# A two-layer graph network on one core: layer 1's projection bias and the experts' gated last biases move from TensorE to VectorE

## The chip, the core and the metric

The kernel runs on one core of a Trainium2 chip. A core has a matrix engine (TensorE, PE in the profile, with its weight loads listed as PEld), a vector engine (VectorE, DVE), a scalar engine (ScalarE, ACT), GpSimd (POOL) and a queue engine (SyncE, SP). Each works through its own list of instructions in order; semaphores make one wait for another. Data lies in main memory (DRAM), in the on-chip memory SBUF (128 partitions) and, for the results of TensorE, in the banks of PSUM. Transfers are issued from SP, ACT or POOL. The metric is the device time of one execution in microseconds (us); lower is better.

## What is computed

Two layers, each of a graph convolution, an attention mix and a feed-forward part, over 3,125 nodes with 256 features and 100,000 edges. The change lies in the second layer ("layer 1"). What matters of the reference there, shortened:

```
xn = layernorm(x)
x  = x + gnn(xn) + mix(xn)
x  = x + experts(layernorm(x))

mix:      y   = second-order attention of 8 heads over all nodes
          mix = y @ Wproj.T + bproj                       # bproj: 256 numbers
experts:  w   = softmax(xl @ Wr + br)                     # 8 gates for each node
          h1  = relu(bn1(xl @ W1[e] + b1[e]))             # for each expert e of 8
          h2  = relu(bn2(h1 @ W2[e] + b2[e]))
          out = sum over e of  w[e] * (h2 @ Wo[e] + bo[e])    # bo: 8 x 256 numbers
```

All of it is in four-byte floating point. `bproj` and `bo` are not zero in the inputs used.

## The kernel before

The nodes lie in 25 tiles of 128 rows (the last has 53), and most loops go over chunks of four tiles (`CHUNKS`; seven, the last of a single tile). The kernel lays the edges out as dense matrices of counts, so that each aggregation over the graph is a product with a 3,125 x 3,125 matrix on TensorE. Layer 1 starts at about 1,300 us. Three of its stages matter here.

*The second aggregation with the queries* (from `layer1_middle`, the block of pools `mid_2`, about 1,700 to 2,023 us). `conv_rows` (L875 to L898) multiplies the matrix's columns, loaded from DRAM on SP's queue (L832) and cast by ScalarE (L835), with the features `hs` that stay in SBUF (L888, 128x512 products). Between these products the generator `queries` (L2085) is advanced step by step by `before(k)`: for each of two groups of heads it multiplies two streams `left` and `right` on VectorE (L2107; both are loaded on POOL's queue at L2082, with 1 MB each) and takes the results to TensorE (L2116). A denominator goes the way L2095, L2098 (VectorE, `ns`), L2099 (ScalarE), L2111 (TensorE, `bp`), L2113 (VectorE, a reciprocal). L2118 puts a group together in `oT`, and then, for each tile, L2125 multiplies with the projection weights into a PSUM bank `yp`, L2126 adds the bias to the same bank, and L2127 adds the bank to the node's row `xc` in SBUF. `xc` was loaded at the chunk's start (L2203, SP's queue). At the end of a chunk `row_sums` (L901, with L906, L907 and L909) adds the aggregation to `xc`, and L2220 stores it.

*The experts' preparation* (`prepare`, L1886). For a chunk it loads `xc` (L1891), normalizes it (L165 to L180), turns it into columns on TensorE (L191 to L195) and computes the eight gates (L1900 to L1917). Then, for each tile, `weighted_bias` (L1039) adds the gated biases: a transpose of the gates on TensorE (L1042), a copy by ScalarE (L1044), a product of the transposed gates with the eight rows `bo` (L1046), and an addition to `xc` by VectorE (L1047). The first chunk is prepared ahead, inside the aggregation's last chunks; the others each during the experts of the chunk before, two steps of the generator per expert from the second expert on.

*The experts* (`experts1`, L1924, from about 2,023 us to the end). Here the chunks are four of four tiles and three of three. For each chunk and each of eight experts: two layers of products over columns (L1952) with ScalarE's activation (L1957), then for each tile a product with the last weights (L1968) into one of three banks, and VectorE's L1971, which multiplies the bank by the tile's gate and adds it to `xc`. At the chunk's end L1977 stores `xc` as the result.

The order on each engine comes from the compiler, which goes by the order of writing and by its own estimate of when an instruction's inputs are there; an instruction whose inputs are there early can be placed far ahead of where it is written. Memory of a pool that has ended is reused, and an instruction that writes there waits for the last reader of the tile that lay there. The weights of experts 1 to 7 are loaded on SP's queue (L1863) when the aggregation's memory comes free.

`bo` is loaded by `common` (L1866) on ACT's queue as 8 rows of 256 numbers; `bproj` lies in `rows`, a block that was copied to all 128 partitions at the start (L1482), and L2126 uses one partition of it.

Of the kernel before, what the change touches and what calls it, by code (L numbers as in the profile page):

```python
# [7 lines left out]
F32 = mybir.dt.float32  # L8
# [4 lines left out]
OP = mybir.AluOpType  # L13
# [4 lines left out]
P = 128  # L18
# [80 lines left out]
def tile_gps_layers(ctx: ExitStack, tc: tile.TileContext, a: dict, out: bass.AP):  # L99
# [1766 lines left out]
    def common(fp):  # L1866

        w_r = load_w(fp, "f1_wr", 2)
        bo = fp.tile([NE1, C], F32, name="bo")
        nc.scalar.dma_start(bo, a["f1_bo"])  # L1870

        bn = []
        for i in "12":
            v = fp.tile([P, 16], F32, name="bn_v" + i)
            DVE.tensor_scalar(v, col("v" + i), 1e-3, None, op0=OP.add)
            sc = fp.tile([P, 16], F32, name="bn_s" + i)
            rsqrt_v(fp, sc, v, [P, 16], "bn" + i)
            DVE.tensor_mul(sc, sc, col("g" + i))
            bi = fp.tile([P, 16], F32, name="bn_b" + i)
            DVE.tensor_sub(bi, col("b" + i), col("m" + i))  # L1880
            DVE.tensor_mul(bi, bi, sc)
            DVE.tensor_add(bi, bi, col("be" + i))
            bn.append((sc, bi))
        return w_r, bo, bn

    def prepare(fw, psp, tag, queue, ts, w_r, bo, got, spare=None):  # L1886


        n = len(ts)
        xc = fw.tile([P, 4, C], F32, name="xc", bufs=1 if spare else 3)  # L1890
        queue.dma_start(xc[:, :n], x_dram[ts[0]:ts[0] + n].rearrange("t p c -> p t c"))  # L1891
        xn = layernorm(fw, [xc[:, i] for i in range(n)], xn=spare and spare())
        yield
        xT = fw.tile([P, 2, 512], F32, name="xT")
        to_columns(psp, tag, xn, ts, xT)
        yield
        gp_ = psp.tile([P, 512], F32, name="gp_", tag=tag)
        for i in range(n):
            for k in range(2):
                PE.matmul(  # L1900
                    gp_[:, i * 8:(i + 1) * 8], xT[:, k, i * P:(i + 1) * P], w_r[:, k, :],
                    start=k == 0, stop=k == 1,
                )
        gate = fw.tile([P, 4, NE1], F32, name="gate")
        ga = gate[:, :n]
        DVE.tensor_add(
            ga, gp_[:, :n * 8].rearrange("p (t e) -> p t e", e=8),
            row("f1_br")[:, None, :].to_broadcast([P, n, 8]),
        )
        red = fw.tile([P, 4], F32, name="red")  # L1910
        DVE.tensor_reduce(red[:, :n], ga, AX.X, OP.max)
        DVE.tensor_sub(ga, ga, red[:, :n, None].to_broadcast([P, n, 8]))
        ACT.activation(ga, ga, AF.Exp)
        yield
        DVE.tensor_reduce(red[:, :n], ga, AX.X, OP.add)
        DVE.reciprocal(red[:, :n], red[:, :n])
        DVE.tensor_mul(ga, ga, red[:, :n, None].to_broadcast([P, n, 8]))  # L1917
        got[:] = xT, gate, xc
        yield
        for i, t in enumerate(ts):  # L1920
            weighted_bias(psp, tag, fw, gate[:, i, :], NE1, bo, xc[:, i])
            yield

    def experts1(pre):  # L1924

        with pool("ffn", **right) as fp, pool("ffn_w", bufs=2, **right) as fw, pool("ps_f", bufs=3, space=PSUM) as ps, \
                pool("ps_fp", bufs=2, space=PSUM) as psp:
            now = []
            chunks = CHUNKS[:4] + [list(range(t, t + 3)) for t in range(16, NT, 3)]
            if pre:  # L1930
                (w_r, bo, bn), got, ws = pre
            else:
                w_r, bo, bn = common(fp)
                got, ws = [], [expert(fp, 0, nc.sync)]
                for _ in prepare(fw, psp, "p", nc.sync, chunks[0], w_r, bo, got):
                    pass
            ws = ws + [expert(fp, e, nc.sync) for e in range(1, NE1)]
            for c, ts in enumerate(chunks):
                xT, gate, xc = got
                w = sum(rows_of(t) for t in ts)  # L1940
                got = []
                ahead = iter(())
                if c + 1 < len(chunks):
                    ahead = prepare(fw, psp, "p", nc.sync, chunks[c + 1], w_r, bo, got)
                for e in range(NE1):
                    h = xT
                    for layer in range(2):
                        hn = fw.tile([P, 2, 512], F32, name=f"h{layer}")
                        for f in range(2):
                            hp = ps.tile([P, 512], F32, name="hp", tag="h")  # L1950
                            for k in range(2):
                                PE.matmul(  # L1952
                                    hp[:, :w], ws[e][layer][:, k, f * P:(f + 1) * P], h[:, k, :w],
                                    start=k == 0, stop=k == 1,
                                )
                            at = 2 * e + f
                            ACT.activation(  # L1957
                                hn[:, f, :w], hp[:, :w], AF.Relu,
                                bias=bn[layer][1][:, at:at + 1], scale=bn[layer][0][:, at:at + 1],
                            )  # L1960
                        h = hn
                    if e:
                        turns(ahead, 2)
                    for i, t in enumerate(ts):
                        r = rows_of(t)
                        yp = ps.tile([P, 512], F32, name="yp", tag="y")
                        for k in range(2):
                            PE.matmul(  # L1968
                                yp[:r, :C], h[:, k, i * P:i * P + r], ws[e][2][:, k, :], start=k == 0, stop=k == 1
                            )  # L1970
                        DVE.scalar_tensor_tensor(  # L1971
                            xc[:r, i], yp[:r, :C], gate[:r, i, e:e + 1], xc[:r, i], op0=OP.mult, op1=OP.add
                        )
                for _ in ahead:
                    pass
                r0, full = ts[0] * P, [t for t in ts if rows_of(t) == P]
                stores = [nc.sync.dma_start(  # L1977
                    out[r0:r0 + len(full) * P, :].rearrange("(t p) c -> p t c", p=P), xc[:, :len(full)]
                )]
                if len(full) < len(ts):  # L1980
                    stores.append(nc.sync.dma_start(out[(NT - 1) * P:N, :], xc[:LAST, len(full)]))
                for o in stores:
                    after(o, stored)
                now.extend(stores)
            stored.extend(now)

    def layer1(fast, rest):
        with pool("l1", **right) as lp:
# [96 lines left out]
            def queries(qw, lq, pst, ps, ts, xc, early):  # L2085
# [3 lines left out]
                for g in range(2):  # L2089
# [15 lines left out]
                    for m in range(4):  # L2105
                        qq = qw.tile([P, 4 * 512], F32, name="qq", bufs=2)
                        DVE.tensor_mul(qq[:, :4 * w], left[m % 2], right[m // 2])  # L2107
                        yield
                        if m == 0:
                            bp = ps.tile([P, 512], F32, name="bp", tag="a")  # L2110
                            PE.matmul(bp[:, :w], sel, ns[:, :w], start=True, stop=True)  # L2111
                            rden = qw.tile([P, 512], F32, name="rden", bufs=1)
                            DVE.reciprocal(rden[:, :w], bp[:, :w])  # L2113
                        for h in range(4):
                            s = slice(h * HD, (h + 1) * HD)
                            PE.matmul(acc[s, :w], kvp[:, g, m, s], qq[:, h * w:(h + 1) * w], start=False, stop=m == 3)  # L2116
                        yield
                    DVE.scalar_tensor_tensor(  # L2118
                        oT[:, g, :w], acc[:, :w], vs[:, g:g + 1], rden[:, :w], op0=OP.add, op1=OP.mult
                    )  # L2120
                    yield
                for i in range(n):
                    yp = ps.tile([P, 512], F32, name="yp", tag="a")
                    for g in range(2):
                        PE.matmul(yp[:, :C], oT[:, g, i * P:(i + 1) * P], wpr[:, g, :], start=g == 0, stop=False)  # L2125
                    PE.matmul(yp[:, :C], ones[0:1, :], row("m1_bproj")[0:1, :], start=False, stop=True)  # L2126
                    DVE.tensor_add(xc[:, i], yp[:, :C], xc[:, i])  # L2127
                    yield

            def layer1_middle(fast, rest, left_, pre):  # L2130
                with pool("mid", **right) as ch, pool("mid_a", bufs=2, **right) as ca:
# [58 lines left out]
                    with pool("mid_2", **right) as cw, pool("ps_c2", space=PSUM) as psc, \  # L2190
# [7 lines left out]
                        for ts in CHUNKS:  # L2198
# [8 lines left out]
                            if fast and ts is CHUNKS[5]:  # L2207
# [1 line left out]
                                made = common(fp)  # L2209
                                got, ws = [], [expert(fp, 0, nc.scalar)]  # L2210
                                spare = lambda: cw.tile([P, 4, C], F32, name="xc", bufs=2)
                                early_work.append(prepare(fp, ps, "a", nc.scalar, CHUNKS[0], *made[:2], got, spare))
                                pre.extend((made, got, ws))
                            acc = conv_rows(ca, psc, hs, ts, fast, gen, before)
                            for _ in work:
# [70 lines left out]
```

## Time and profile before

| | |
|---|---|
| median of 3 runs | 2601.89 us (2598.73 to 2609.38) |
| profiled execution | 2595.34 us, of which the span of the instructions is 2593.4 us |
| mean granted TensorE clock | 0.970 |
| from 2046 us to the end: L1968, L1952 on TensorE | 774 records, 188.4 us; 864 records, 351.0 us |
| the same: L1971 on VectorE | 195, 92.7 us, 482 ns each |
| the same: L1046 on TensorE | 42 records, 14.6 us |
| the same: L1047 on VectorE | 21, 8.9 us, 425 ns each |
| L2126 on TensorE, 1746.4 to 2020.9 us | 50 records, 374 to 791 ns, median 478 |

The times of the runs are of executions without a profile; the profiled execution is another one, and sums made from the trace are compared with its own time. A product of four-byte numbers shows as two records on TensorE, each with a weight load; records of consecutive products overlap, so the time that a product holds TensorE is read from the starts, not from the sum of the durations. In lists of groups, `out<-in` names the tiles written and read, and idle time is put down to what ended it ("<-PE yp L1968": the engine waited for that product).

### The profile page before, as it was taken

What the parts mean: (1) busy time and instruction counts of PE and PEld (TensorE: products, weight loads), DVE (VectorE), ACT (ScalarE), POOL (GpSimd) and SP (SyncE); (2) the same over time, 40 slices, a digit from 0 to 9 for tenths busy, and PEclk for the clock granted to TensorE, in tenths of its full rate; (3) what the DMA queues carried; (4) which work ended last, traced back from release to release, by engine and by line L of the source; (5) the groups of instructions that cost most, each with busy time, mean ns of one, the idle gap of its engine ahead of it and who ended that gap; (6) DMA issues with size and microseconds to landing.
All of it is one profiled execution on the core that took longest, in us unless ns stands there. A gap on an engine that the chain in (4) does not pass through costs nothing.

```text
span 2593.4 us, 33233 instructions
## 1 busy us (share of the span) xinstructions
PE 2442.5 (94%) x12351; PEld 1531.6 (59%) x12351; DVE 1545.2 (60%) x3534; ACT 1382.0 (53%) x2356; POOL 145.2 (6%) x203
## 2 busy tenths in 40 slices
PE   5788999989997999999999899989999999999998
PEld 3466777666674545555564576755555555555665
DVE  5689976548848777766778565566775412222221
ACT  5756766569858898777745334343332232222332
POOL 5320000000000000000001000001110000000000
PEclk9899999989997899999999999998999999999999
DMA  6434444366643211111146644387873400000000
GB/s 192 137 102 154 162 160 154 128 204 240 225 133 107 68 51 56 57 57 48 51 140 220 223 150 136 94 297 265 295 286 116 130 8 1 15 15 9 8 5 13
DMA packets 197059, 318.44 MB, mean 123 GB/s; under 512 B 12461, under 2 KB 171510, under 8 KB 190742
## 3 DMA queue, kind: packets, MB, share of 16 engines
q1 hardware_dynamic: 177110, 246.11, 29.2%
q0 software_dynamic: 14592, 64.28, 7.0%
q10 hardware_dynamic: 5184, 5.82, 0.7%
q8 instruction: 99, 1.62, 0.3%
q14 instruction: 74, 0.61, 0.1%
HBM read 229.40 MB, written 86.73 MB: 122 GB/s over the span
## 4 chain that ended last, share of the span: by engine, by line
PE 66%; DMA 5%; DVE 4%; ACT 3%; issue 1%; POOL 0%; ACTq 0%; DVEq 0%; SPq 0%; POOLq 0%
PE hp L1952 13%; PE acc L888 9%; PE yp L1968 7%; PE yp L1132 7%; PE hp L1118 6%; PE acc L862 6%; PE qa L2038 2%; PE by_s L1284 2%; PE tt L2116 2%; DMA adj<-cols 2%; PE wb_p L1046 1%; PE by_a L1282 1%; PE b_bank L419 1%; DMA xs_n<-hs_dram 1%; ACT adj_r L835 1%
## 5 line engine op out<-in xcount | busy, mean ns | idle before, releaser
L835 ACT CAST adj_r<-adj 128x2560 fp32r<-128x2560 bf16 (+1 forms) x140 | 293.6, 2104 | 303.2 <-PE acc L862 114.1
L888 PE MATMUL acc<-hs,adj_r 128*128 128x512 f32 (+1 forms) x1250 | 360.1, 421 | 14.4 <-ACT adj_r L835 11.6
L1957 ACT ACTIVATE h<-hp,bn_b,bn_s 128x512 f32<-128x512 f32 (+2 forms) x224 | 160.9, 723 | 368.6 <-PE hp L1952 368.6
L862 PE MATMUL acc<-adj_r,hs 128*128 128x512 f32 (+1 forms) x1400 | 353.9, 395 | 0.5 <-ACT adj_r L835 0.5
L1271 ACT ACTIVATE pos<-drow,a_s 128x512 bf16<-128x512 f32 (+2 forms) x532 | 311.5, 665 | 0.9 <-PE by_s L1284 0.5
L888 PEld LDWEIGHTS acc<-hs,adj_r 128*128 128x128 f32 (+1 forms) x1250 | 226.8, 190 | 114.7 <-issue 55.9
L1971 DVE SCALAR_TENSOR_TENSOR xc<-yp,gate,xc 128x256 f32<-128x256 f32 (+1 forms) x200 | 95.1, 482 | 320.5 <-PE yp L1968 320.3
L862 PEld LDWEIGHTS acc<-adj_r,hs 128*128 128x128 f32 x1400 | 245.9, 191 | 55.6 <-issue 8.3
L1118 PE MATMUL hp<-g_xT,w 128*128 128x512 f32 (+2 forms) x448 | 199.1, 563 | 1.9 <-issue 1.6
L1132 PE MATMUL yp<-w,hT 128*128 128x256 f32 x800 | 196.3, 387 | 0.0
L1968 PE MATMUL yp<-w_f_wo,h 128*128 128x256 f32 (+1 forms) x800 | 194.7, 386 | 0.3 <-ACT h L1957 0.2
L1275 DVE TENSOR_TENSOR pos<-pos,adj 128x2048 bf16<-128x2048 bf16 (+2 forms) x133 | 147.0, 1105 | 67.9 <-ACT pos L1271 67.6
L1952 PE MATMUL hp<-h,w_f_w 128*128 128x512 f32 (+2 forms) x448 | 185.8, 545 | 0.3
L2029 DVE TENSOR_TENSOR kk<-vk 128x512 f32<-128x512 f32 (+1 forms) x200 | 125.3, 687 | 99.1 <-issue 51.6
L436 ACT CAST b_stage<-b_bank 128x500 bf16<-128x500 f32 (+8 forms) x363 | 169.2, 534 | 27.6 <-PE b_bank L419 25.9
L1952 PE MATMUL hp<-xT,w_f_w 128*128 128x512 f32 (+2 forms) x448 | 181.9, 544 | 1.6 <-issue 1.6
L390 DVE TENSOR_TENSOR b_ul<-lo_b,upto 128x2048 bf16<-128x2048 bf16 x117 | 148.9, 1273 | 48.3 <-PE b_bank L419 48.0
L1968 PEld LDWEIGHTS yp<-w_f_wo,h 128*128 128x128 f32 (+1 forms) x800 | 142.6, 187 | 49.8 <-ACT h L1957 14.5
L1132 PEld LDWEIGHTS yp<-w,hT 128*128 128x128 f32 x800 | 147.8, 191 | 40.6 <-issue 20.0
L419 PE MATMUL b_bank<-b_uh,b_ul 128*128 128x125 bf16 (+5 forms) x1856 | 138.7, 214 | 17.6 <-DVE b_uh L395 10.4
L419 PEld LDWEIGHTS <-b_ul 128*128 128x128 bf16 x1856 | 101.8, 100 | 67.4 <-issue 48.8
L1952 PEld LDWEIGHTS hp<-h,w_f_w 128*128 128x128 f32 x448 | 81.6, 189 | 94.0 <-issue 38.8
(563 smaller groups left out, 3382.1 us busy)
## 6 DMA issues: line engine op xcount, KB each, us to landing
adj<-cols SPq DMA_DIRECT2D x145, 640.0 KB, 4.4
cols<-b_stage SPq DMA_DIRECT2D x50, 800.0 KB, 3.6
left<-q_dram POOLq DMA_DIRECT2D x22, 1024.0 KB
right<-q_dram POOLq DMA_DIRECT2D x20, 1024.0 KB
xs_n<-hs_dram SPq DMA_DIRECT2D x15, 640.0 KB, 5.5
vk<-vk_dram SPq DMA_DIRECT2D x10, 840.0 KB, 5.5
vk_dram<-vk SPq DMA_DIRECT2D x6, 1344.0 KB, 4.9
x_in<-in_x SPq DMA_DIRECT2D x12, 512.0 KB, 3.9
```

Of the source, the lines that this page charges most:

```text
L390: DVE.tensor_tensor(u, lo[:, s].rearrange("p (m j) -> p m j", j=2)[:, :, None, :].to_broadcast([P, group // 2, P, 2]), upto[:, None, :P, : ...
L419: PE.matmul(bank[:, n * NT:(n + w) * NT], u[:, i // 2, :, i % 2], v[:, i // 2, :NT * w, i % 2], start=k == 0, stop=k == room - 1,)
L436: ACT.copy(dst, src)
L835: ACT.copy(dst, src)
L862: PE.matmul(acc[f][:, :w], hs[:, k, q, s], at[k - k0][:, :len(ts)], start=k == 0 and q == 0, stop=k == NT - 1 and q == 1,)
L888: PE.matmul(acc[i][:r, :], at[k - k0][:, i, :r], hs[:, k].rearrange("p q c -> p (q c)"), start=k == 0, stop=k == NT - 1,)
L1118: PE.matmul(hp[:, :w], w1[:, e, k, f * P:(f + 1) * P], xT[:, k, c0:c0 + w], start=k == 0, stop=k == 1)
L1132: PE.matmul(yp[:, :C], hT[:, f, i * P:(i + 1) * P], w2[:, e, f, :], start=f == 0, stop=f == 3)
L1271: ACT.activation(pos[:, h, :n].rearrange("p t d -> p (t d)"), drow[:, h, :w], AF.Sign, bias=a_s[:, k, h:h + 1],)
L1952: PE.matmul(hp[:, :w], ws[e][layer][:, k, f * P:(f + 1) * P], h[:, k, :w], start=k == 0, stop=k == 1,)
L1957: ACT.activation(hn[:, f, :w], hp[:, :w], AF.Relu, bias=bn[layer][1][:, at:at + 1], scale=bn[layer][0][:, at:at + 1],)
L1968: PE.matmul(yp[:r, :C], h[:, k, i * P:i * P + r], ws[e][2][:, k, :], start=k == 0, stop=k == 1)
```

## The change

Two biases are no longer products.

The projection bias: the product L2126 goes, so that L2125 alone fills the bank. In its place VectorE adds the 256 numbers of `bproj`, which lie in every partition of `rows`, to all tiles of the chunk's `xc` in one operation, written after the first group's last product and ahead of its L2118.

The gated biases: the loop over `weighted_bias` at the end of `prepare` goes. `bo` is now loaded in `experts1` on POOL's queue as one row of 8 x 256 numbers copied to all 128 partitions (8 KB in each), as the first tile of the experts' pool. Before each expert's products VectorE multiplies the bias row of the expert before with its gate and adds it to `xc`, one operation for each tile; the last expert's turn adds its own row too.

```diff
     def common(fp):
         w_r = load_w(fp, "f1_wr", 2)
-        bo = fp.tile([NE1, C], F32, name="bo")
-        nc.scalar.dma_start(bo, a["f1_bo"])
...
     def prepare(fw, psp, tag, queue, ts, w_r, got, spare=None):
...
         got[:] = xT, gate, xc
         yield
-        for i, t in enumerate(ts):
-            weighted_bias(psp, tag, fw, gate[:, i, :], NE1, bo, xc[:, i])
-            yield
 
     def experts1(pre):
...
+            bo = fp.tile([P, NE1, C], F32, name="bo")
+            nc.gpsimd.dma_start(
+                bo.rearrange("p e c -> p (e c)"),
+                a["f1_bo"].rearrange("(o e) c -> o (e c)", o=1).to_broadcast([P, NE1 * C]),
+            )
...
                 for e in range(NE1):
+                    for b in {0: (), NE1 - 1: (e - 1, e)}.get(e, (e - 1,)):
+                        for i in range(len(ts)):
+                            DVE.scalar_tensor_tensor(
+                                xc[:, i], bo[:, b], gate[:, i, b:b + 1], xc[:, i], op0=OP.mult, op1=OP.add
+                            )
                     h = xT
...
+                    if not g:
+                        DVE.tensor_add(xc[:, :n], xc[:, :n], row("m1_bproj")[:, None, :].to_broadcast([P, n, C]))
                     DVE.scalar_tensor_tensor(
                         oT[:, g, :w], acc[:, :w], vs[:, g:g + 1], rden[:, :w], op0=OP.add, op1=OP.mult
                     )
...
                     for g in range(2):
-                        PE.matmul(yp[:, :C], oT[:, g, i * P:(i + 1) * P], wpr[:, g, :], start=g == 0, stop=False)
-                    PE.matmul(yp[:, :C], ones[0:1, :], row("m1_bproj")[0:1, :], start=False, stop=True)
+                        PE.matmul(yp[:, :C], oT[:, g, i * P:(i + 1) * P], wpr[:, g, :], start=g == 0, stop=g == 1)
                     DVE.tensor_add(xc[:, i], yp[:, :C], xc[:, i])
```

The rest of the diff passes `bo` no longer from `common` to `prepare` and `experts1`.

More of the change, by code (lines that the diff above doesn't have):

```diff
@@ L1883, in common, with prepare @@
             bn.append((sc, bi))
-        return w_r, bo, bn
-    def prepare(fw, psp, tag, queue, ts, w_r, bo, got, spare=None):
+        return w_r, bn
+    def prepare(fw, psp, tag, queue, ts, w_r, got, spare=None):
         n = len(ts)
@@ L1929, in experts1 @@
             chunks = CHUNKS[:4] + [list(range(t, t + 3)) for t in range(16, NT, 3)]
+            bo = fp.tile([P, NE1, C], F32, name="bo")
[3 more added lines that the diff above has]
+            )
             if pre:
-                (w_r, bo, bn), got, ws = pre
+                (w_r, bn), got, ws = pre
             else:
-                w_r, bo, bn = common(fp)
+                w_r, bn = common(fp)
                 got, ws = [], [expert(fp, 0, nc.sync)]
-                for _ in prepare(fw, psp, "p", nc.sync, chunks[0], w_r, bo, got):
+                for _ in prepare(fw, psp, "p", nc.sync, chunks[0], w_r, got):
                     pass
@@ L1943, in experts1 @@
                 if c + 1 < len(chunks):
-                    ahead = prepare(fw, psp, "p", nc.sync, chunks[c + 1], w_r, bo, got)
+                    ahead = prepare(fw, psp, "p", nc.sync, chunks[c + 1], w_r, got)
                 for e in range(NE1):
+                    for b in {0: (), NE1 - 1: (e - 1, e)}.get(e, (e - 1,)):
[3 more added lines that the diff above has]
+                            )
                     h = xT
@@ L2211, in layer1_middle @@
                                 spare = lambda: cw.tile([P, 4, C], F32, name="xc", bufs=2)
-                                early_work.append(prepare(fp, ps, "a", nc.scalar, CHUNKS[0], *made[:2], got, spare))
+                                early_work.append(prepare(fp, ps, "a", nc.scalar, CHUNKS[0], made[0], got, spare))
                                 pre.extend((made, got, ws))
```

## The prediction

> **What bounds the kernel now.** I read the page's busy shares first, then the stretches of the two stages that the change touches, then the chain of work, and last the single lines. The page:
>
> ```profile
> PE 2442.5 (94%) x12351; PEld 1531.6 (59%) x12351; DVE 1545.2 (60%) x3534; ACT 1382.0 (53%) x2356; POOL 145.2 (6%) x203
> ```
>
> The share is an average, so the stages decide. Busy time by stretch (start:end, length, then PE, PEld, DVE, ACT, POOL, clock, DMA share, GB/s); the first two are chunks of layer 1's second aggregation, the last two lie in its experts:
>
> ```profile
> 1852.15:1900.52 48.37, 48.37 (x205) 26.41 (x205) 32.72 (x26) 15.42 (x13) 5.74 (x10) 1.00 0.80 286
> 1900.52:1948.89 48.37, 48.37 (x206) 26.40 (x205) 32.63 (x26) 15.42 (x13) 5.73 (x10) 1.00 0.75 275
> 2100.00:2200.00 100.00, 99.88 (x317) 55.36 (x316) 20.14 (x47) 28.82 (x41) 0.00 (x0) 1.00 0.02 6
> 2200.00:2300.00 100.00, 99.89 (x312) 54.31 (x310) 22.84 (x64) 29.38 (x42) 0.00 (x0) 1.00 0.03 10
> ```
>
> TensorE never rests in either stage; VectorE is busy 68% in the aggregation and 20 to 23% in the experts. Work taken from TensorE there is time, work given to VectorE is time only where TensorE waits for it. The chain of the experts (start, duration, piece) starts an expert every 10.87 us (2178.09 to 2188.96 to 2199.83), but 12.52 to 12.56 us where bias steps lie in it:
>
> ```profile
> 2153.01 4.29 PE hp L1952 x10
> ...
> 2165.53 4.29 PE hp L1952 x10
> ...
> 2178.09 4.29 PE hp L1952 x10
> ...
> 2188.96 4.29 PE hp L1952 x10
> ...
> 2199.83 4.29 PE hp L1952 x10
> ```
>
> The same chain close up shows what the extra time is:
>
> ```profile
> 2160.15 0.11 PE wb_t L1042
> 2160.26 1.46 PE yp L1968 x6
> 2161.72 0.62 PE wb_p L1046 x2
> 2162.34 0.20 PE wb_t L1042
> 2162.55 0.43 PE yp L1968 x2
> 2162.98 0.62 PE wb_p L1046 x2
> ```
>
> The projection bias, in TensorE's order of one chunk (each product of four-byte numbers is two records):
>
> ```profile
> 1893.12 1.02 PE L2125 MATMUL yp<-w_m_wproj,oT 128*128 128x256 f32 x4
> 1894.07 0.69 PE L2126 MATMUL yp<-rows,ones 1*128 1x256 f32 x2
> 1894.70 0.50 PE L888 MATMUL acc<-hs,adj_r 128*128 128x512 f32 x1
> ```
>
> L2126 holds TensorE from 1894.07 to 1894.70, 0.63 us, though it has one row.
>
> **The change part by part.** Time removed in the experts: L1042, L1044, L1046, L1047 for 21 tiles after 2023. Chunks of four tiles prepare a chunk of four in two experts of 12.52 and 12.56 instead of 10.87 us: 3.34 us, three times, 10.0. The fourth prepares three tiles: its two experts run from 2337.23 to 2361.44, 24.21 less 21.74, 2.5 us. A chunk of three tiles takes 7.75 us per expert without bias; from 2402.45 to 2469.69 it took 67.24 us, less 62.0, less 0.66 for transposes and 1.24 for gates, leaves 3.3, of which I count 3.2, twice: 6.4. Together 18.9 us, all on a chain that is TensorE's alone.
>
> The first chunk's four bias steps run in the aggregation, near 1989 to 2005, 0.62 and 0.11 us each: 2.9 us.
>
> The projection bias is 25 products. The chain's own list for 1745 to 2023 (278 us) gives L2126 4.6%, that is 12.8 us: 17 at 0.62, two at 1.15 in a stretch of slow clock. The other six lie in the first two chunks, where the chain goes through a load of the matrix (17.22 us from 1737.81) and one of POOL's (12.02 us from 1781.28); I count them as nothing, since those loads hide them. If that cover is gone they are worth 6 x 0.62 = 3.7 us. Next behind L2125 stand L888, which waited for its casts 3.3 us in this whole stage, and L2127, which now waits for L2125. A tile of this loop goes from 1.92 to 1.29 us, against 0.42 us of L2127, so the two banks of yp don't hold it.
>
> Removed: 12.8 + 2.9 + 18.9 = 34.6 us.
>
> Added, (a): seven additions of the projection bias, six over 1,024 elements per partition. The rows of the same kind are 0.42 us at 256 (L907), 0.69 at 512 and 2.29 at 2,048 (L2107): a line through the last two gives 1.22 us. Written just ahead of L2118, but the trace runs VectorE's work well ahead of its place: the layernorm that is written in the sixth chunk ran at 1787, in the second. So the addition goes to a gap after the load of xc, a chunk ahead (issued 1867.31, 1915.64). Gaps of 2.5 to 3.4 us before L2113 hold it for nothing. If it falls between L2118 and L2098 instead, it delays ns, for which TensorE already waits:
>
> ```profile
> PEld bp L2111 <- ACT ns L2099: 4.8, 7, 0.8
> ```
>
> (line, what is waited for, us in total, times, longest). Then up to 1.2 us a chunk are lost: ends 0 and 7.3 us. I take 0.9 in two chunks of six, 1.8, being nearer to the gaps, which are longer than the work. The four L1047 that go here give VectorE back 1.7 us.
>
> (b): the eight bias rows copied to all partitions, 1 MB on POOL's queue in place of 8 KB on ACT's (0.38 us of ACT's issue, hidden). It is the first tile of the experts' memory, where hs lay, so it waits for the last L888 at 2021.87; POOL's last load before it is issued at 2012.56 and nothing is queued behind it. The nearest rows: a row block copied to all partitions at the start, 836 KB, landed in 8.4 us, which makes 10.5 for 1 MB; POOL's own 1 MB took 12.02. So it lands at 2032 to 2034; the first addition that needs it follows L1971 of expert 0, at 2034.7. At best it costs nothing. At worst it shares the queues until the burst of weights ends (5.4 MB and 1.5 MB of xc, 350 GB/s until 2044, with 1 MB more until 2047): VectorE stands for 12 us, L1971 behind it frees no bank and TensorE stands at the fourth yp. The same megabyte makes xc of the next chunks land up to 2.9 us later, and there TensorE waited already 0.36 us for ln_xn at 2052. I take 1.5 us, half of that, since the likelier lands in time.
>
> (c): 200 additions over 256 elements, 0.42 (L907) to 0.48 us (L1971), 90 us of VectorE in 562. In an expert of 10.87 us there are then 1.9 us of L1971 and 1.9 us of these (3.8 in the last expert), and 5 us of layernorm in one of eight. Between two yp of 0.93 us VectorE has at worst 1.44 us of work, so it falls 1.5 us behind over four tiles, and TensorE needs the next bank 7 us later. Nothing on the path; if that cover were gone, it is 0.5 us in each of the 56 experts, 28 us. Each addition waits for gate and xc, both there since L1971 of the expert before; queued behind it stand L1971 and the next layernorm. TensorE's loads and ScalarE's 21 copies L1044 go for nothing, being beside TensorE.
>
> Sum: 34.6 - 1.8 - 1.5 = 31.3 us. The profiled execution took 2595.3 us (span 2593.4), so it would be 2564.0. That execution lies 6.6 us under the median of the runs, 2601.9; against the median I forecast **2570 us**.
>
> [...] Row first: POOL's issues of left and right take 0.53 to 0.55 us whether L2107, an operation with two inputs from SBUF, is running (1839.45) or not (1783.47). [...]
>
> **The rivals.** 1: slower or nothing gained. The additions (a) run ahead to where the compiler thinks xc has landed, and VectorE stands in order until it has. For it speaks a row of today, where a layernorm that ran ahead did this:
>
> ```profile
> 1787.18 0.43 DVE L165 BATCH_NORM_STATS2 ln_st<-xc 128x6 f32<-128x256 f32 x1 [3.84 <-DMA xc<-x_dram]
> ```
>
> The longest such wait, in the experts, was 6.4 us. Against it: VectorE rests 15.6 of 48.37 us in a chunk, and the wait counts only where it falls ahead of L2098 or of the first qq. Its price is the wait and 1.2 us in each of seven chunks, in place of the 1.8 above; it decides from 33.1 / 7 = 4.7 us a chunk. At 3.84 us it is 35 us, 2604; at 6.4 us 53 us, 2601.9 - 33.1 + 53 = 2622; at half of the smaller, 2587.
>
> 2: the aggregation doesn't become faster, because loads set its pace once the products go. For it: 286 GB/s and 80% in a chunk, and waits of qq for left, 7.3 us in five. Against: a chunk 2.5 us shorter asks 302 GB/s, and the weights ran at 350. Then only the experts and the four early steps are gained: 2601.9 - 21.8 + 3.3 = 2583.
>
> [...]
>
> 4: the order in the experts lets TensorE wait for yp banks after all, 0.3 us (as L1971 does today in 14 cases) in most experts, 15 us: 2585.
>
> **How the numbers follow.** Forecast 0.72; rival 1 0.09, of which 0.05 with the longer wait; rival 2 0.12; rival 3 0.03; rival 4 0.04. Low end: all products and steps on the path, 34.6 + 3.7 = 38 us, and no cost, off the lowest run 2598.7, is 2560; 3 us less for scatter, 2557. High end: 34.6 - 7.3 - 12 = 15 us off the median is 2587, which holds rivals 2 to 4 at their own times; 2 us more for scatter, 2589. About 0.5%, 13 us, is what a measurement can tell from no change, so faster is under 2589: the forecast, 0.10 of rival 2 (whose reach goes past that), rival 3 and half of rival 4, 0.87. Slower is rival 1 with the longer wait, 0.05. The same has the rest, 0.08. The forecast's own range is 2560 to 2583.
>
> **What would show it.** Right: no L2126 and no wb lines; a chunk of the aggregation at 45.9 us with TensorE still full; every expert of four tiles after the gates at 10.87 us; VectorE near 36 to 39% in the experts. Wrong: VectorE idle before the new addition with xc's load as releaser; bp waiting for ns more than 0.8 us; a hole in TensorE between 2034 and 2050 (in the new times some 14 us earlier) with the load of the bias rows behind it; left or right as releaser of qq for longer than 3.4 us.

## The result and the profile after

The changed kernel takes 2577.18 us (median of 4 runs, 2574.97 to 2579.05) beside 2600.31 us for the kernel before on the same chip (4 runs, 2598.09 to 2609.38). The ratio is 0.9893, with a 95% interval of 0.9874 to 0.9912: about 1.1% faster. Forecast were 2570 us and a range of 2557 to 2589. The profiled execution of the changed kernel is one of its four runs (2574.97 us), and so it is with every kernel of the experiments; only the kernel before was profiled in an execution of its own.

In the profile of the changed kernel the lines of the code have moved: the projection is L2134, its addition L2135, the new addition of the projection bias L2126, `ns` L2105 and L2106, `bp` L2118, `xc`'s load L2211; in the experts the new additions are L1950, the products L1959 and L1975, and `bo`'s load L1927. The page's busy shares:

```profile
span 2573.0 us, 33018 instructions
PE 2398.4 (93%) x12226; PEld 1518.1 (59%) x12226; DVE 1617.1 (63%) x3716; ACT 1377.2 (54%) x2331; POOL 145.7 (6%) x204
```

TensorE has lost 44 us of work and is no fuller than before. So I cut the span at two events that both kernels have, the first query product (`gq`) and the first product of expert 0. Busy time by stretch (start:end, length, then PE, PEld, DVE, ACT, POOL, clock, DMA share, GB/s); the first row is the aggregation, the second the experts. Before:

```profile
1699.10:2023.50 324.40, 316.24 (x1374) 174.26 (x1373) 215.93 (x242) 101.31 (x101) 34.48 (x60) 0.97 0.71 247
2023.50:2593.40 569.90, 561.50 (x1885) 331.00 (x1885) 137.09 (x392) 169.23 (x257) 0.00 (x0) 0.99 0.07 21
```

After:

```profile
1703.30:2022.75 319.45, 290.78 (x1312) 166.96 (x1311) 219.36 (x245) 100.97 (x97) 34.99 (x61) 0.95 0.72 250
2022.75:2573.00 550.25, 541.16 (x1822) 325.59 (x1822) 206.06 (x571) 165.17 (x236) 0.00 (x0) 1.00 0.07 24
```

The experts are 19.65 us shorter. The aggregation is 4.95 us shorter, though TensorE has 25.5 us less to do in it: its idle time in this stretch went from 8.2 to 28.7 us. Everything ahead of 1700 us is the same code and happened to take 4.2 us longer in this execution. Together that is the 20.4 us by which the two profiled executions differ (2595.3 and 2575.0).

The chain of the experts after (start, duration, piece) answers the forecast line by line. An expert starts every 10.87 us, and the experts that had carried bias steps do so too:

```profile
2159.26 4.29 PE hp L1959 x10
...
2170.13 4.29 PE hp L1959 x10
...
2181.00 4.29 PE hp L1959 x10
...
2191.87 4.29 PE hp L1959 x10
```

Two stretches inside the experts show that VectorE has room for the 200 additions: it is busy 34 to 36% of the time and TensorE still never rests.

```profile
2100.00:2200.00 100.00, 99.87 (x313) 56.06 (x314) 33.76 (x83) 28.80 (x38) 0.00 (x0) 1.00 0.02 6
2200.00:2300.00 100.00, 99.87 (x313) 56.07 (x314) 36.22 (x101) 28.81 (x38) 0.00 (x0) 1.00 0.06 19
```

The aggregation is where the profile differs from the forecast. VectorE's own order around the addition for the fourth chunk (start, duration, engine, line, operation; in brackets the idle time ahead of it and what ended it):

```profile
1830.15 0.74 DVE L2127 SCALAR_TENSOR_TENSOR oT<-tt,vs,rden 128x512 f32<-128x512 f32 x1
1840.30 1.23 DVE L2126 TENSOR_TENSOR xc<-xc,rows 128x1024 f32<-128x1024 f32 x1 [9.41 <-DMA xc<-x_dram]
1841.44 2.28 DVE L2114 TENSOR_TENSOR qq<-left,right 128x2048 f32<-128x2048 f32 x1
1843.64 0.74 DVE L2105 SCALAR_TENSOR_TENSOR ns<-gq,ksum,q 128x512 f32<-128x512 f32 x1
```

And TensorE's at the same place:

```profile
1836.15 1.05 PE L2123 MATMUL tt<-qq,kvp 128*32 128x512 f32 x2
1845.10 2.08 PE L2118 MATMUL bp<-ns,sel 128*128 128x512 f32 x2 [7.91 <-ACT ns L2106]
```

The compiler put the fourth chunk's bias addition right behind the `oT` of the third chunk's first group, ahead of the `qq` and `ns` of its second. Its operand `xc` had been asked for at 1828.36 (SP's row of L2211) and came at 1840.30. VectorE works in order, so it stood for 9.41 us, and `ns`, which TensorE needs for `bp`, came late: TensorE stood for 7.91 us. The list of waits for 1690 to 2025 us (line, what is waited for, us in total, times, longest) has five such waits. It also tells where TensorE's 20.5 us of additional idle time went, namely to two waits in about equal parts:

```profile
DVE xc L2126 <- DMA xc<-x_dram: 26.0, 5, 9.4
PE bp L2118 <- ACT ns L2106: 9.7, 4, 7.9
PE acc L888 <- ACT adj_r L835: 13.5, 2, 7.9
```

In the kernel before no product `bp` waited for `ns`; for the cast matrix there was this much:

```profile
PE acc L888 <- ACT adj_r L835: 4.1, 2, 2.9
```

### The profile page after: what moved, and what is told of

Its sections match the earlier page's. It is cut to its first block, busy times and chain, and to the rows that moved or that the text cites. A ratio compares the mean times of both kernels' runs of the same rounds, so it can differ in the third digit from the quotient of the medians.

```text
span 2573.0 us, 33018 instructions
## 1 busy us (share of the span) xinstructions
PE 2398.4 (93%) x12226; PEld 1518.1 (59%) x12226; DVE 1617.1 (63%) x3716; ACT 1377.2 (54%) x2331; POOL 145.7 (6%) x204
## 5 line engine op out<-in xcount | busy, mean ns | idle before, releaser
L888 PE MATMUL acc<-hs,adj_r 128*128 128x512 f32 (+1 forms) x1250 | 361.1, 421 | 24.0 <-ACT adj_r L835 21.0
L888 PEld LDWEIGHTS acc<-hs,adj_r 128*128 128x128 f32 (+1 forms) x1250 | 226.7, 189 | 117.9 <-issue 49.1
L1975 PE MATMUL yp<-w_f_wo,h 128*128 128x256 f32 (+1 forms) x800 | 190.7, 384 | 0.3 <-ACT h L1964 0.2
L1959 PE MATMUL hp<-h,w_f_w 128*128 128x512 f32 (+2 forms) x448 | 185.6, 545 | 0.3
L436 ACT CAST b_stage<-b_bank 128x500 bf16<-128x500 f32 (+8 forms) x363 | 169.2, 534 | 28.7 <-PE b_bank L419 25.7
L1959 PE MATMUL hp<-xT,w_f_w 128*128 128x512 f32 (+2 forms) x448 | 180.8, 539 | 1.6 <-issue 1.6
L1975 PEld LDWEIGHTS yp<-w_f_wo,h 128*128 128x128 f32 (+1 forms) x800 | 144.9, 187 | 48.1 <-issue 12.3
L419 PE MATMUL b_bank<-b_uh,b_ul 128*128 128x125 bf16 (+5 forms) x1856 | 138.9, 214 | 17.4 <-DVE b_uh L395 10.2
L1959 PEld LDWEIGHTS hp<-h,w_f_w 128*128 128x128 f32 x448 | 81.7, 189 | 94.4 <-issue 38.3
```

Source lines behind the costliest of these rows:

```text
L419: PE.matmul(bank[:, n * NT:(n + w) * NT], u[:, i // 2, :, i % 2], v[:, i // 2, :NT * w, i % 2], start=k == 0, stop=k == room - 1,)
L436: ACT.copy(dst, src)
L888: PE.matmul(acc[i][:r, :], at[k - k0][:, i, :r], hs[:, k].rearrange("p q c -> p (q c)"), start=k == 0, stop=k == NT - 1,)
L1959: PE.matmul(hp[:, :w], ws[e][layer][:, k, f * P:(f + 1) * P], h[:, k, :w], start=k == 0, stop=k == 1,)
L1975: PE.matmul(yp[:r, :C], h[:, k, i * P:i * P + r], ws[e][2][:, k, :], start=k == 0, stop=k == 1)
```

## The experiments

The theory after the result: the experts' part is worth what was forecast, and of the projection's part most is lost to this wait, by what it exceeds TensorE's slack. Rivals: the load of `xc` and the others set the aggregation's pace once the products go (the prediction's rival 2); the additions themselves cost VectorE's time on the path (step (a)'s upper end); or the lost time lies in the profiled execution alone.

**The parts alone.** `agg_only` keeps the experts as before and changes the projection alone; `exp_only` does the reverse.

```diff
 # agg_only, against the kernel before
+                    if not g:
+                        DVE.tensor_add(xc[:, :n], xc[:, :n], row("m1_bproj")[:, None, :].to_broadcast([P, n, C]))
...
-                    PE.matmul(yp[:, :C], ones[0:1, :], row("m1_bproj")[0:1, :], start=False, stop=True)
...
 # exp_only, against the changed kernel
-                    if not g:
-                        DVE.tensor_add(xc[:, :n], xc[:, :n], row("m1_bproj")[:, None, :].to_broadcast([P, n, C]))
...
+                    PE.matmul(yp[:, :C], ones[0:1, :], row("m1_bproj")[0:1, :], start=False, stop=True)
```

> The kernel before with the experts' part of the change alone: the products of the gated biases go, the projection bias stays a product. Theory W and the forecast's terms alike: 18.9 us of the experts and 2.9 of the first chunk, less 1.5 for the load of the rows: 20.3 us faster, 2578 to 2582, and the experts from their first product to the end take 550 us as in the changed kernel. If the experts' part too hides a loss, it is under 17 us.

Measured: ratio 0.9921 (0.9898 to 0.9943), 2583.94 us beside 2605.79, or 20.6 us less by the ratio. The forecast's steps for this part are 18.9 + 2.9 - 1.5 = 20.3 us. Its experts take 550.88 us, its aggregation 321.72, 2.7 us less than before (the four early steps).

> The kernel before with the projection part of the change alone: the product of one row goes, the VectorE addition comes where the change has it; the experts' biases stay products. Theory W: the products removed give 12.8 us, the waits take 8 to 11 of them back: 2 to 5 us faster than the kernel before, 2595 to 2599. Rival L: 0 to 2 us. The forecast's own terms: 11 us faster, 2589.

Measured: ratio 0.994 (0.9922 to 0.9959), 2589.98 us, some 15.6 us less. The expectation from the theory missed: in this comparison the part gains what the prediction gave it (12.8 - 1.8 = 11 us) or more. Its aggregation took 307.89 us, yet VectorE waited for `xc` here too, in the same five places. The waits were shorter, though (17.8 us together in place of 26.0), and TensorE stood for only 3.2 us at `bp`. The addition of the fourth chunk, and `bp` behind it:

```profile
1831.27 1.23 DVE L2119 TENSOR_TENSOR xc<-xc,rows 128x1024 f32<-128x1024 f32 x1 [2.15 <-DMA xc<-x_dram]
1836.07 1.13 PE L2111 MATMUL bp<-ns,sel 128*128 128x512 f32 x2 [1.32 <-ACT ns L2099]
```

**The addition left out, and the addition moved.** Both ran on the same chip as the two above. `no_add` drops the new addition, so its result lacks the projection bias; `late_add` writes it behind the chunk's last L2135, where `xc` has been waited for anyway.

```diff
 # no_add has only the first three lines, late_add the whole
-                    if not g:
-                        DVE.tensor_add(xc[:, :n], xc[:, :n], row("m1_bproj")[:, None, :].to_broadcast([P, n, C]))
                     DVE.scalar_tensor_tensor(
...
                     DVE.tensor_add(xc[:, i], yp[:, :C], xc[:, i])
                     yield
+                DVE.tensor_add(xc[:, :n], xc[:, :n], row("m1_bproj")[:, None, :].to_broadcast([P, n, C]))
+                yield
```

> The changed kernel without its VectorE addition of the projection bias: layer 1's projection bias is left out, nothing takes its place. Theory W (the additions stand in VectorE's order ahead of the landing of xc and hold it up): the waits of 18.9 us go, the aggregation takes some 11 us less than in the changed kernel, about 309 us from its first query product to the first expert product in place of 319.4, and the time is 2563 to 2568. Rival L (the loads of matrix and streams set the aggregation's pace, so that products removed there are worth nothing): no change against the changed kernel, 2575 to 2579, and TensorE's waits for the cast matrix stay above 13 us.

> The changed kernel with the same additions written behind the last addition of yp of the chunk, which they must wait for, so that they can't run ahead. Theory W: the waits for xc go; each addition of 1.22 us now stands ahead of the chunk's y_lo additions, costing at most 1.2 us a chunk, 0 to 7 us in all: 2564 to 2573, and VectorE waits for no load of xc in the aggregation. Rival L: 2575 to 2579 as the changed kernel. Rival D (the price is the 1.22 us of work on VectorE and not the wait): no better than the changed kernel.

Measured: `no_add` 0.986 (0.984 to 0.9879), `late_add` 0.9865 (0.9846 to 0.9885). Their aggregations (start:end, length, busy times and shares as above), first without the addition, then with it written late:

```profile
1701.30:2009.87 308.57, 291.20 (x1312) 166.65 (x1311) 212.45 (x238) 100.36 (x97) 34.94 (x61) 0.96 0.76 260
```

```profile
1701.80:2010.15 308.35, 291.73 (x1312) 166.39 (x1311) 221.11 (x245) 100.71 (x97) 35.00 (x61) 0.98 0.75 261
```

Seven additions, 7.8 us of VectorE's time (six of 1.22 to 1.23 and one of 0.43), cost nothing when they wait for nothing. The removal of the projection's products and of the four early steps is worth 15.8 us of aggregation (324.40 - 308.57), so loads do not set the pace of the stage as a whole: the same megabytes move at 260 instead of 247 GB/s. The profiled aggregation of the changed kernel is 11 us longer than either. That of `agg_only` (307.89 us) is a little shorter still, though it waits for `xc` and has the four early steps in it; TensorE waited 7.0 us for the cast matrix there and 8.7 in `no_add`, which accounts for a part only. So executions of this stage differ by some microseconds for other reasons too. Two whole chunks of `late_add`:

```profile
1852.00:1897.09 45.09, 45.09 (x197) 25.58 (x196) 33.86 (x28) 16.06 (x15) 5.73 (x10) 1.00 0.83 299
1897.09:1942.19 45.10, 45.10 (x197) 25.57 (x196) 33.86 (x27) 15.51 (x13) 5.73 (x10) 1.00 0.80 292
```

A chunk takes 45.1 us with TensorE full, beside 48.37 before.

**The addition's price with the products kept, and the addition held at its place.** These ran on another chip, with the changed kernel and the late addition again beside them. `zero_add` is the kernel before with VectorE adding a row of zeros where the change adds the bias. `held_add` is the changed kernel with a factor of 1.0 made from `oT`, so that the addition can't be placed ahead of the chunk's own `oT`.

```diff
 # zero_add, against the kernel before
+            nil = lp.tile([P, C], F32, name="nil")
+            DVE.memset(nil, 0.0)
...
+                    if not g:
+                        DVE.tensor_add(xc[:, :n], xc[:, :n], nil[:, None, :].to_broadcast([P, n, C]))
 # held_add, against the changed kernel (in place of its addition, and behind oT)
+                    if not g:
+                        one = qw.tile([P, 1], F32, name="one", bufs=1)
+                        DVE.tensor_scalar(one, oT[:, g, 0:1], 0.0, 1.0, op0=OP.mult, op1=OP.add)
+                        DVE.scalar_tensor_tensor(
+                            xc[:, :n], row("m1_bproj")[:, None, :].to_broadcast([P, n, C]), one, xc[:, :n], op0=OP.mult, op1=OP.add
+                        )
```

> The kernel before, whose products all stay, with the changed kernel's additions in the aggregation put in as well, but of a row of zeros: the added operations and their waits alone, the result unchanged. Theory W: VectorE waits 15 to 26 us for xc, and the kernel is 2 to 10 us slower than before. If neither the waits nor the work come onto the path: 0 to 2 us slower. [...]

> The changed kernel with the additions at the place where they are written, but multiplied with a number (1.0) that is made from the group's own oT, so that they can't run ahead of L2127 (a small operation of about 0.15 us more in each chunk). They then stand between oT and ns of the next group. Theory W: no wait for xc, up to 1.2 us a chunk of later ns where TensorE waits for it: 0 to 8 us slower than late_again. Rival D (the work at this place is the price): 8 us or more slower than late_again.

> The changed kernel once more, beside the next one on one chip. The part alone (agg_only) had the same waits of VectorE for xc, 17.8 us in five, but none longer than 7.7, and lost little; the changed kernel had one of 9.41 us ahead of ns with TensorE standing 7.91 us behind it. Theory W, as it stands now (the price of a wait is what it exceeds TensorE's slack by, and the landing of xc differs from execution to execution): 22 to 30 us faster than the kernel before and 5 to 12 us slower than late_again; the aggregation between 308 and 320 us, with the difference to 308 found again as TensorE's wait for ns and for the cast matrix. If the 9.41 us were one accident: within 3 us of late_again.

> The kernel late_add once more (the projection bias added behind the chunk's last yp), on the same chip as the changed kernel. Theory W: 34 to 36 us faster than the kernel before, aggregation 308 to 310 us. Accident: the same as after_again within 3 us.

Measured, beside 2588.93 us for the kernel before on that chip: `zero_add` 1.0026 (1.0004 to 1.0047), `held_add` 0.9839 (0.9813 to 0.9865), the changed kernel 0.9842 (0.9817 to 0.9866), the late addition 0.9847 (0.9823 to 0.9871). In `zero_add` the addition, alone, costs 0.26%, about 7 us (1 to 12), and its profile has the wait and the hole behind it at the place known by now:

```profile
1823.92 1.23 DVE L2121 TENSOR_TENSOR xc<-xc,nil 128x1024 f32<-128x1024 f32 x1 [7.91 <-DMA xc<-x_dram]
1828.73 2.07 PE L2113 MATMUL bp<-ns,sel 128*128 128x512 f32 x2 [6.36 <-ACT ns L2101]
```

In the profiles the held and the late addition have no wait for `xc` and aggregations of 311.09 and 309.57 us, the changed kernel 317.54. But the three times are the same. So the expectation that the changed kernel would be slower than the late addition missed in the times and held in the profiles.

**Once more, on a third chip**, to tell "the wait differs from execution to execution" from "something in the experts' part makes `agg_only` differ". The three kernels are the changed one, the late addition and `agg_only`, unaltered.

> The changed kernel as it is, a third time, beside the same kernel with the bias addition written behind the chunk's last projection. Theory (the addition runs ahead of the load of xc, and the wait costs what exceeds TensorE's slack): in the profile VectorE waits for xc ahead of the bias addition, some 18 to 26 us in five places, TensorE has a hole of 2 to 8 us at a bp or an acc behind it, the aggregation lasts 316 to 320 us, and the time is 5 to 11 us above that of the late addition. Rival (what the profiles show is in the profiled executions alone): the times of the two lie within 3 us.

> The bias addition behind the chunk's last projection, a third time. Theory: no wait of the bias addition for xc, the aggregation lasts 308 to 310 us, the time is 5 to 11 us below the changed kernel's on this chip. Rival: within 3 us of it.

> The projection's part alone, again: the one kernel that had the waits of VectorE for xc and an aggregation as short as without them. If the wait costs what exceeds TensorE's slack, and that differs from execution to execution: an aggregation between 308 and 320 us that goes up with the longest wait of a bp for ns, and a time 8 to 18 us below the kernel before. If something of the experts' part makes the difference: 308 us again, with holes of bp for ns under 2 us.

Measured, beside 2602.64 us for the kernel before: the changed kernel 2569.2 us, 0.987 (0.9848 to 0.9892); the late addition 2565.53 us, 0.9853 (0.9831 to 0.9875); `agg_only` 2593.77 us, 0.996 (0.9945 to 0.9974). The profiled aggregations were 321.39, 309.10 and 330.32 us. Between the changed kernel and the late addition, 5 to 11 us had been expected and, by the rival, under 3; the 3.7 us measured fall between the two, and the intervals overlap. `agg_only` gains 10.4 us by the ratio here, inside the 8 to 18 expected, but its aggregation is longer than the 308 to 320 us expected. That number settles the question for `agg_only`: the same program had 307.89 us in the execution profiled first, so nothing in its text makes it immune. In the second execution the waits were long, and this is the third of them with its hole:

```profile
1841.93 1.23 DVE L2119 TENSOR_TENSOR xc<-xc,rows 128x1024 f32<-128x1024 f32 x1 [8.96 <-DMA xc<-x_dram]
1846.74 2.07 PE L2111 MATMUL bp<-ns,sel 128*128 128x512 f32 x2 [7.41 <-ACT ns L2099]
```

That execution took 2610.47 us, and the other six of the same kernel 2590.05 to 2597.67. The profiled executions of the changed kernel tell less: each has about 9 us of holes at `bp` (9.7, 8.7 and 9.8, of which 0.7 to 1.4 stand behind no wait for `xc`). But against the median of the other runs beside it, that of the result is 3.6 us faster, and the two later ones are 8.9 and 8.7 us slower. So on the two later chips long holes look like an exception among the runs, and on the chip of the result they don't.

Put side by side, the waits for `xc` ahead of the additions of the fourth, fifth and sixth chunk (two where there were two) and the holes behind them, in the same order:

| execution | VectorE's wait, us | TensorE's hole at `bp`, us |
|---|---|---|
| changed kernel | 9.41, 2.05, 2.23 | 7.91, 0.49, 0.67 |
| again | 6.56, 3.83, 1.38 | 5.00, 2.27, none |
| third | 8.34, 3.10 | 6.85, 1.54 |
| `zero_add` | 7.91, 1.02, 0.92 | 6.36, none, none |
| `agg_only` | 2.15, 3.48, 1.36 | 1.32, 1.92, none |
| `agg_only` again | 8.96, 4.93, 5.57 | 7.41, 3.38, 4.01 |

The hole is the wait less 1.5 us, and a wait under 1.5 us leaves none; the first wait of `agg_only` (2.15) is the one that doesn't follow. The waits ahead of these, at the additions of the first and the third chunk, meet other work: the longest, 10.23 us in the third execution of the changed kernel, let TensorE's projection wait 6.03 us for `oT`.

## Why the prediction was right, and where it was not

*The experts, 18.9 us, and the early steps, 2.9.* Right. `exp_only` gave 20.6 us where these steps less the load's price make 20.3. In the profiled execution the experts became 19.65 us shorter; 1.7 us of it is chance, since the first expert's first products took 5.37 us before, at a granted clock of 0.70 (2023.50 to 2025.50) and 0.50 (2025.50 to 2027.50), and 3.67 us after, at 1.00. A three-tile chunk takes 64.0 us (2388.68 to 2452.68) where it took 67.24.

*The load of the bias rows, 1.5 us (0 to 12).* Near its lower end. It was issued on POOL's queue at 2021.41, the first addition ran at 2032.58 and waited for nothing; the next chunk's columns on TensorE waited 0.83 us for the layernorm at 2051.85 instead of 0.36. The rows of the load and of the 200 additions (engine and line; for the second count, ns min/median/max, first and last start):

```profile
2021.41 0.54 POOL L1927 DMA_DIRECT2D bo<-in_f_bo  x1 [8.74 <-DVE xc L2135]
```

```profile
L1950 DVE SCALAR_TENSOR_TENSOR xc<-bo,gate,xc x200: 466/477/486, 2032.6 to 2560.0; 128x256 f32<-128x256 f32 x100
```

*The additions in the experts, nothing.* Right: 477 ns each, and no product of TensorE waited for a bank; its weight loads did for 2.3 us in seven cases, where before it had been 4.6 us in fourteen. Rival 4 falls.

*The projection's products, 12.8 us.* Right as a sum, by two errors that cancel. A tile of the projection takes 1.09 us, not the forecast 1.29:

```profile
1999.86 1.02 PE L2134 MATMUL yp<-w_m_wproj,oT 128*128 128x256 f32 x4
2000.53 0.58 PE L888 MATMUL acc<-hs,adj_r 128*128 128x512 f32 x1
2000.95 1.03 PE L2134 MATMUL yp<-w_m_wproj,oT 128*128 128x256 f32 x4
```

The product was worth 1.92 - 1.09 = 0.83 us, not the 0.63 between two starts, because the product ahead of it holds TensorE for a shorter time when L2126 doesn't follow it (0.67 instead of 0.95 us to the next start); why it does is not shown. So a chunk is 45.1 and not 45.9 us. Against that, TensorE now waits longer for the casts: L888 for `adj_r` 9.0 us in `late_add` between 1715 and 1995, where it was 4.1 before. The early steps of the chunk prepared ahead (2.9) and these two make the 15.8 us that `no_add` shows, where 12.8 + 2.9 = 15.7 had been summed. That the errors have the same size is luck.

*Step (a), 1.8 us with ends of 0 and 7.3: the step whose mechanism failed.* The sentence is "So the addition goes to a gap after the load of xc, a chunk ahead". The additions did run ahead, but into the time before the load had landed, which is rival 1's mechanism, given 0.09. The row that spoke for it (VectorE's 3.84 us ahead of a layernorm) was the right row to read: nothing in that order protects an operation that is placed early. The rival's price was wrong the other way. It charged the whole wait in each of seven chunks, 35 us at the wait of 3.84 us that the trace had shown; in fact the first 1.5 us of a wait cost nothing, since TensorE had that much work left, and the waits that go far beyond it come in one to three chunks. The three profiled executions of the changed kernel have aggregations 8 to 13 us longer than those of the late addition (319.45, 317.54 and 321.39 against 308.35, 309.57 and 309.10). The holes at `bp` are what all three have and the late addition hasn't (9.7, 8.7 and 9.8 us against 0.5, 0.2 and 0.5); the waits for the cast matrix go either way (13.5, 5.4 and 4.7 against 9.0, 10.2 and 6.6).

Over all runs the price is smaller. The changed kernel and the late addition differ by -0.05% on one chip and +0.17% on the other (about -1 and +4 us), with intervals that overlap; `zero_add` puts the addition's price at 1 to 12 us. Which of these holds for a typical execution of the changed kernel stays open: only one run of each kernel carries a trace, and the 1.8 us forecast lies inside what the times allow. That the sum came out close although this step went another way than forecast is in part luck.

*Rivals 2 and 3.* Rival 2 falls by `no_add` and `late_add` for the stage as a whole. It holds in one place, near the end of the second chunk, where L888 stands longer for the cast of a matrix load that lands late: 1.26 us before, 5.05 in `no_add` and 6.77 in `late_add`. That additions hold up POOL's loads, to which the chances give 0.03 as rival 3, no run shows: POOL's 61 issues take 35.00 us in the late addition's aggregation where 60 took 34.48 before, 0.57 us each on average in both kernels, and the additions there cost nothing.

*The sum.* Forecast was 31.3 us, a ratio of 0.988. The three comparisons of the changed kernel gave 0.9893, 0.9842 and 0.987; 0.988 lies inside the intervals of the first and the third and above that of the second, which reaches to 0.9866. The 7 us between 2577 and 2570 are therefore no more than one comparison differs from the next. What would have mattered more for the mechanism was to look for the landing time of `xc` before giving rival 1 its chance: its issue and its first reader were both in the trace.

No version here is measurably faster than the changed kernel. The late addition is the safer text, since its profiles have no wait for `xc` ahead of `bp`.

## What to carry to other kernels

Before an operation is added to an engine with idle time, look whether its inputs are there when its turn in that engine's order comes. Here the same seven additions cost nothing where they waited for nothing (an aggregation of 308.35 us, 308.57 without them) and the profiled aggregations were 8 to 13 us longer where they stood ahead of a load (waits of up to 10.23 us). Where the compiler sets the order by its own estimate of a load, write the operation behind something that needs the same load anyway. Price a wait on an engine off the path by what it exceeds the slack of the engine that waits for the work queued behind it (1.5 us at `bp` here); read that slack from the trace, and count the excess only at the places where there is one. Profile a kernel more than once before a single hole is counted as its time: `agg_only` had 3.2 us of holes at `bp` in one execution and 14.8 in another.

## What the runs showed of the hardware

The fourth chunk's load of `xc`, 512 KB issued on SP's queue among the loads of the matrix and the query streams, landed 6.0 us after its issue in one execution of `agg_only` (issued 1825.25, used 1831.27) and 12.1 us in another on another chip (1829.81 and 1841.93). The place in the program is the same, so a landing time from one trace is one sample.

Two holes of TensorE cost more than their length. After the 7.91 us hole of the changed kernel the granted clock (the third column from the end) was 0.50 for 4.6 us, up to 1849.70:

```profile
1845.10:1847.10 2.00, 2.00 (x2) 0.50 (x2) 0.00 (x0) 0.00 (x0) 0.64 (x1) 0.50 0.88 287
1847.10:1849.10 2.00, 2.00 (x8) 0.33 (x7) 1.88 (x1) 0.00 (x0) 0.00 (x0) 0.50 0.72 259
1849.10:1851.10 2.00, 2.00 (x11) 0.67 (x12) 2.00 (x2) 0.00 (x0) 0.00 (x0) 0.84 0.26 102
1851.10:1853.10 2.00, 2.00 (x9) 1.65 (x10) 2.00 (x2) 0.00 (x0) 0.09 (x1) 1.00 0.06 16
```

By the granted clock the first 6 us did the work of 3.7, so 2.3 us more were lost. The same stood behind the shortest of the slowed holes at `bp`, 2.27 us in the second execution of the changed kernel (the hole itself, then what followed):

```profile
1869.43:1871.70 2.27, 0.00 (x1) 0.00 (x1) 2.27 (x3) 0.63 (x1) 0.53 (x1) 0.88 1.06 364
1871.70:1873.70 2.00, 2.00 (x3) 0.83 (x3) 1.48 (x1) 0.00 (x0) 0.23 (x1) 0.50 1.04 296
1873.70:1875.70 2.00, 2.00 (x10) 0.20 (x8) 1.89 (x1) 0.00 (x0) 1.02 (x2) 0.50 0.98 377
1875.70:1877.70 2.00, 2.00 (x8) 1.43 (x5) 2.00 (x2) 0.00 (x0) 0.00 (x0) 0.50 0.96 395
```

There the loss at 0.50, 3 us in the 6.0 us shown, is more than the hole. Behind all holes at `bp` from 2.27 us up the two `bp` products take 2.07 or 2.08 us, behind those up to 1.92 us 1.12 or 1.13. No single length divides the holes that were followed by a lower clock from the others. The 1.64 us hole ahead of the first expert was followed by slow products in two profiles, the kernel before and `zero_add` (eight records of products in 5.37 and 5.15 us), and by fast ones in the five others that have it (3.67 us). Behind holes of 2.19 us (`late_add`, up to 1740.95) and 2.29 us (`zero_add`, up to 1753.71) the products were fast: three records of L888 in 0.97 us and eight in 2.06. From 2.36 us up, every hole in the rows listed from the profiles (between 1,689 and 1,950 us) had slow products within a microsecond behind it: behind 2.36 us in the changed kernel, up to 1702.61, the clock was 0.50 from 1703.10 to 1705.60, and behind 2.38 us in its third execution, up to 1743.80, three records of L888 took 1.65 us. What decides below that is not shown.

So at these places VectorE's wait cost TensorE nothing up to 1.5 us, its excess from there, and 2.3 and 3 us on top behind the two holes shown, 7.91 and 2.27 us long.
